# Small memsets between GpSimd's additions, and a new pace for the additions on weights

## The chip, the cores and the metric

The kernel runs on one core of one Trainium2 chip. The metric is the device time of one execution in microseconds (us), the median of several runs. The kernel before took 2261.07 us (median of 3 runs, 2245.42 to 2261.88).

Engines are named as in the profile: PE is TensorE's matmul, PEld its weight load, DVE is VectorE, ACT is ScalarE, POOL is GpSimd, SP is SyncE, whose queue issues nearly all DMAs here. "L141" is line 141 of the kernel file.

## What is computed

Two layers with residuals on `x` of 2 sequences x 2048 tokens x 512, all float32:

```
def _L0_cond_ref(...):
    s0 = relu(x @ swi[0]) @ swo[0]
    s1 = relu(x @ swi[1]) @ swo[1]
    wi_sel = wi[type_label]; wo_sel = wo[type_label]     # one expert per sequence
    h  = relu(einsum('bsd,bdf->bsf', x, wi_sel))
    eo = einsum('bsf,bfd->bsd', h, wo_sel)
    gate_in = concatenate([eo[:, 0], s0[:, 0], s1[:, 0]], -1)
    w = softmax(relu(gate_in @ g1) @ g2)                 # three weights per sequence
    return eo * w[:, 0] + s0 * w[:, 1] + s1 * w[:, 2]

x = x + _L0_cond_ref(...)
x = x + (x @ W[cat_ids] + b[cat_ids])
```

The inner widths are 512 and 2048. Nearly all work lies in the pairs of products `x @ wi` and `h @ wo`.

## The kernel before

**Units and stages.** The tokens are cut into 4 blocks of 1024. A unit is one dense pair on one block: shared expert 0 on four blocks (units 0 to 3), shared expert 1 on four blocks (units 4 to 7), then the chosen expert of sequence 0 (units 8 and 9) and of sequence 1 (units 10 and 11). Each unit has two stages: `up` (the product with `wi`, PE line L803) and `down` (the product with `wo`, PE line L938). Below, "up3" is the up stage of unit 3. In units 9, 10 and 11 the second layer of the blocks that are ready is woven in.

**Products with fewer multiplications.** Every product is done by a two-level Strassen-Winograd scheme: seven outer products instead of eight, and in each of them seven inner ones. Each stage has therefore 49 inner products, of 8 matmuls of 128x256 each: 392 matmuls. The price is sums of blocks of the operands and of the results. Three kinds matter here:

- *Sums on weights* (class `Prep`, additions at L141 through `sums_a`). For each of the six pairs (expert 1, 2, 3) x (wi, wo) there are four groups of 12 additions: four that make `po` (128x384), four `ps` and four `pt` (128x512), read from a raw tile `pr` that four pairs of DMAs load (L179). The sums are stored to DRAM (L228) and loaded later as weights. That is 288 additions on POOL. The sums of expert 0 are made in unit 0 by another class (`First`, L549 and L625), partly on DVE and partly on POOL; the change does not touch it.
- *Sums of x* (`x_sums`, additions at L366 by `outer` and at L380 by `inner`). 36 POOL instructions for each of the units in `MAKES` (0 to 4); PE reads the results (`xi`, `xt`) as moving operands in the same unit's up stage. Units 5 and later load them from DRAM.
- *Sums of h and of the results* on DVE, such as L738 to L745, L781, L909 and L915, whose two inputs both lie in SBUF, and L826 to L850 or L960 to L971, which read one input from PSUM.

**What sets the order.** The schedule is written out by hand: each engine's instructions run in the order in which the program issues them. A stage `up` walks through seven outer products (index `j`, 0 to 6) of 14 slots each; a slot is four matmuls, some 0.86 us of PE time. In each slot the program may issue one step of the sums of x (`advance(xg, 1)`), and then calls `prep_paced(RATE_UP[j])`: the rate is added to a balance (`pace`, at most 4) and each whole unit of the balance issues one addition on weights. With `RATE_UP` (0.36 or 0.24 per slot) a stage issues up to 14 x 2.28 = 31.9 of them. In `down` the rate is 0, and `prep_run` issues two additions at three chosen places (`RUN_DN`); ahead of them it lets POOL wait for a one-element memset of DVE's (`pulse`, L685, read at L686), so that they do not run ahead of their place.

POOL itself knows nothing of slots: it takes its list in order as fast as the data allow. The first addition of each group of 12 waits for its raw tile and for the store of the group before. The raw loads stand in SP's queue between the loads of weight tiles (L479 to L498), which run 12 tiles ahead of PE.

**The x sums in `up`**, by outer product: during `j`=0 the sums for the second outer product are made, during `j`=1 those for the third, and so on; the last (`inner(3)`, used at `j`=6) is issued in slots 7 to 10 of `j`=5.

Of the kernel before, what the change touches and what calls it, by code (L numbers as in the profile page):

```python
# [8 lines left out]
F32 = mybir.dt.float32  # L9
# [6 lines left out]
P = 128  # L16
# [20 lines left out]
def cond_resid_kernel(  # L37
# [22 lines left out]
    nc = tc.nc  # L60
    B, S, D = x.shape
    E, _, F = wi.shape
# [8 lines left out]
    const = ctx.enter_context(tc.tile_pool(name="const", bufs=1))  # L71
# [59 lines left out]
    def sums_a(eng, pick, put):  # L131


        a11, a12, a21, a22 = pick(0, 0), pick(1, 0), pick(0, 1), pick(1, 1)
        for o, i0, i1, op in (
            (put(5), a21, a22, ADD),
            (put(7), a11, a21, SUB),
            (put(6), put(5), a11, SUB),
            (put(3), a12, put(6), SUB),
        ):  # L140
            eng.tensor_tensor(o, i0, i1, op)  # L141
            yield

    class Prep:


# [8 lines left out]
        def begin(self):  # L155
            if not self.todo:
                return
            g = self.todo.pop(0)
            self.since = clock[0]
            e, kind = self.e, self.kind  # L160
            t = bigp.tile([P, 2048], F32, tag="raw", bufs=1, name=f"pr_{e}_{kind}_{g}")

            raw = t.rearrange("p (q b d f) -> p q b d f", q=4, b=2, d=2)
            cols = slice(g * P, (g + 1) * P)
            for c in range(DC):
                if kind == 0 and e < 2:
                    src = swi_v[:, e * DC + c, :, cols]
                elif kind == 0:
                    src = wi_v[:, bass.ds(label[e - 2] * DC + c, 1), :, cols]
                    src = src.rearrange("p o r f -> p (o r) f")  # L170
                elif e < 2:
                    src = swo_v[:, e * 4 + c, g, :].rearrange("p (r f) -> p r f", r=4)
                else:
                    src = wo_v[:, bass.ds(label[e - 2] * 4 + c, 1), g, :]
                    src = src.rearrange("p o (r f) -> p (o r) f", r=4)
                src = src.rearrange("p (c d) f -> p c d f", c=2)
                a, b = divmod(c, 2)
                for k, q in enumerate((1, 2) if a else (0, 3)):
                    nc.sync.dma_start(out=raw[:, q, b, :, :], in_=src[:, k, :, :])  # L179
            place = lambda n: SLOT_A[n] - 4  # L180
            quad = {(0, 0): 0, (1, 0): 1, (1, 1): 2, (0, 1): 3}
            own = {}

            def view(part):
                if part not in own:
                    self.flush(1 << 30, part)
                    own[part] = bigp.tile(
                        [P, 1536 if part == "o" else 2048], F32, tag=part, bufs=1,
                        name=f"p{part}_{e}_{kind}_{g}",
                    )  # L190
                form = {
                    "s": "p (s b d f) -> p s b d f",
                    "o": "p (q s f) -> p q s f",
                    "t": "p (n s f) -> p n s f",
                }[part]
                return own[part].rearrange(form, s=4, f=P, **({"b": 2} if part == "s" else {}))

            def line(part, pick, put):
                gen = sums_a(nc.gpsimd, pick, put)

                def op(k):
                    next(gen)
                    if part != "t":
                        self.reading -= 1
                        self.free = clock[0] + 3
                    if k == 3:
                        self.late.append((clock[0] + 3, part, g, own[part]))

                return [lambda k=k: op(k) for k in range(4)]

            self.p += line(
                "o", lambda r, c: raw[:, 0:3, r, c, :], lambda n: view("o")[:, :, place(n), :]
            )
            self.p += line(
                "s", lambda r, c: raw[:, quad[r, c]], lambda n: view("s")[:, place(n)]
            )
            self.p += line(
                "t", lambda r, c: view("s")[:, :, r, c], lambda n: view("t")[:, :, place(n)]
            )
            self.reading = 8  # L220
# [13 lines left out]
        def step(self):  # L234

            self.flush(clock[0])
            done = self.can()
            if done:
                self.p.pop(0)()
            self.more()  # L240
            return done
# [116 lines left out]
    def x_sums(n):  # L358

        v = [t.rearrange("p b (c d) f -> p b c d f", c=2) for t in xraw[n]]  # L360
        b11, b12, b21, b22 = (v[r][:, :, c] for r in range(2) for c in range(2))
        new = lambda k: topp.tile([P, 4, TQ], F32, tag="top", name=f"x{k}_{n}")

        def outer(o, i0, i1):
            for b in range(2):
                nc.gpsimd.tensor_tensor(o[:, b], i0[:, b], i1[:, b], SUB)  # L366
                yield

        def inner(i, quad):
            t = new(f"i{i}")  # L370
            s = lambda k: t[:, SLOT_B[k] - 4, :]
            pk = lambda r, c: quad[:, r, c, :]
            for k, i0, i1 in (
                (5, pk(0, 1), pk(0, 0)),
                (6, pk(1, 1), s(5)),
                (7, pk(1, 1), pk(0, 1)),
                (4, pk(1, 0), s(6)),
            ):
                x_ops[n, i, k] = s(k)
                nc.gpsimd.tensor_tensor(s(k), i0, i1, SUB)  # L380
                yield
            for k, (r, c) in {1: (0, 0), 2: (1, 0), 3: (1, 1)}.items():
                x_ops[n, i, k] = quad[:, r, c, :]
            parts_of[n, i] = (quad, t)

        sq = lambda t: t.rearrange("p (b d) f -> p b d f", b=2)
        yield from inner(1, b11)
        yield "next"
        if n == 0:
            yield from inner(2, b21)  # L390
            yield "next"
        t1, t2 = sq(new("t1")), sq(new("t2"))
        yield from outer(t1, b12, b11)
        yield from outer(t2, b22, t1)
        yield from inner(6, t2)
        yield "next"
        if n:
            yield from inner(2, b21)
            yield "next"
        yield from inner(5, t1)  # L400
        yield from outer(b12, b22, b12)
        yield "next"
        yield from inner(7, b12)
        yield from outer(b21, b21, t2)
        yield "next"
        yield from inner(4, b21)
        yield "next"
        yield from inner(3, b22)
        yield "next"


    MAKES, LEAVES = range(NB + 1), range(1, NB + 1)
# [239 lines left out]
    def prep_step():  # L652
        done = prep_bg[0].step()
        if prep_bg[0].over():
            prep_bg.pop(0)
        return done
# [3 lines left out]
    def prep_paced(rate):  # L660
        clock[0] += 1
        if prep_bg:
            prep_bg[0].flush(clock[0])
        pace[0] = min(pace[0] + rate, 4.0) if prep_bg else 0.0
        while prep_bg and pace[0] >= 1 and prep_step():
            pace[0] -= 1

    PULSES = 64
    pulse = const.tile([1, PULSES], F32, name="pulse")
    seen = const.tile([1, 1], F32, name="seen")  # L670
    pulses, debt = [0], [0]

    def prep_run(count):

        if not prep_bg:
            return
        debt[0] = min(debt[0] + count, 4) if count else 0
        most = count + 1
        ready = False
        while prep_bg and debt[0] and most:  # L680
            if prep_bg[0].can() and not ready:
                k = pulses[0] % PULSES
                pulses[0] += 1
                mark = pulse[:, k : k + 1]
                nc.vector.memset(mark, 0.0)  # L685
                nc.gpsimd.tensor_tensor(seen, mark, mark, ADD)  # L686
                ready = True
            if not prep_step():
                break
            debt[0] -= 1  # L690
            most -= 1
# [56 lines left out]
    def up(n, xg, tops, y):  # L748
# [12 lines left out]
        for j, i in enumerate(I_UP(n)):  # L761
# [32 lines left out]
            for s, (bk, k, d) in enumerate(SEQ_UP):  # L794
# [76 lines left out]
                    done = advance(xg, 1)  # L871
                if s in top_at:
                    next(tg, None)
                prep_paced(RATE_UP[j])
                if n or j or s >= 4:
                    step(other_bg)
                if s == 4 and n not in MAKES and j + 2 < NP:
# [9 lines left out]
    def down(n, H, tops, y, prepare):  # L887
# [124 lines left out]
        for s, (i, name) in enumerate(SLOTS_DN):  # L1012
# [12 lines left out]
            prep_paced(0.0)  # L1025
            prep_run(RUN_DN.get((i, name), 0))
            step(other_bg)
# [195 lines left out]


    RATE_UP = [0.36, 0.36, 0.36, 0.36, 0.24, 0.24, 0.36]
    RUN_DN = {(7, "x6"): 2, (4, "x6"): 2, (4, "y5"): 2}

    with tc.manual_schedule():
# [18 lines left out]
        for n, (e, blk) in enumerate(units):  # L1247
# [4 lines left out]
            if n:  # L1252
                y = yp.tile([P, DC, 4, TQ], F32, tag="y", name=f"y_{n}")
            H = up(n, xg, tops, y)
            coming = {}

# [82 lines left out]
```

## Time and profile before

| | |
|---|---|
| median of 3 runs | 2261.07 us (2245.42 to 2261.88) |
| the profiled execution | 2258.7 us, of which the span of the program is 2256.9 us |
| PE busy | 2196.7 us, 9808 matmuls |
| DVE busy | 1647.6 us |
| POOL busy | 753.6 us, 616 instructions |
| granted TensorE clock, mean | 0.995 |

The span is one execution as the hardware profiler recorded it, from the first instruction to the last; 1.8 us of the execution's own time lie around it. A timeline row gives start, length, engine, line, operation, output and inputs, and in brackets how long the engine had been idle before and what ended that.

### The profile page before, as it was taken

The page shows a single profiled execution, that of the slowest core. Times are in us where ns is not written, and L with a number is a line of the kernel's source. Part 1 is how long each engine was busy: PE and PEld are TensorE (multiplying, and loading weights), DVE is VectorE, ACT ScalarE, POOL GpSimd, SP SyncE. Part 2 cuts the span into 40 slices and gives each one's busy share as a digit, 9 for nine tenths or more (in the row PEclk, how much of TensorE's full clock was granted, in tenths as well). Part 3 has the DMA queues.
Part 4 walks back from the last instruction along what each step waited for, and adds up shares of the span by engine and source line. Part 5 has one row for each costly group of instructions (what it writes and reads, how often), then busy time and mean ns, then how long its engine had stood idle before and what let it go on. Part 6 is the DMA issues. An engine that isn't in the chain of part 4 may idle for free.

```text
span 2256.9 us, 28576 instructions
## 1 busy us (share of the span) xinstructions
PE 2196.7 (97%) x9808; PEld 1850.6 (82%) x9808; DVE 1647.6 (73%) x2028; ACT 544.4 (24%) x937; POOL 753.6 (33%) x616
## 2 busy tenths in 40 slices
PE   8899998999999999999999999999999999999999
PEld 6787887888888878888888888888777877887786
DVE  7897778587688597587587687587676746767685
ACT  3321230331231231131141141131133133113310
POOL 5787523550850750240350340330032023002300
PEclk9999999999999999999999999999999999999999
DMA  9553996997997896896897896895896597579671
GB/s 339 202 182 119 340 305 204 306 320 239 306 328 231 284 321 191 295 312 207 297 311 217 270 335 213 277 339 173 294 292 189 186 315 232 152 245 321 212 276 56
DMA packets 483339, 577.22 MB, mean 256 GB/s; under 512 B 28280, under 2 KB 316024, under 8 KB 479740
## 3 DMA queue, kind: packets, MB, share of 16 engines
q1 hardware_dynamic: 479468, 568.58, 77.4%
q10 hardware_dynamic: 3728, 6.82, 0.9%
q8 instruction: 80, 1.31, 0.2%
q14 instruction: 63, 0.52, 0.1%
HBM read 417.47 MB, written 157.81 MB: 255 GB/s over the span
## 4 chain that ended last, share of the span: by engine, by line
PE 61%; DVE 5%; DMA 2%; POOL 1%; issue 0%; ACT 0%; SPq 0%; DVEq 0%; POOLq 0%; ACTq 0%
PE dx L938 18%; PE ux L803 14%; PE dy L938 9%; PE uy L803 7%; PE po L1119 5%; PE dz L938 5%; PE uz L803 3%; DVE h L781 1%; DMA w<-ws_s 1%; DMA g1raw<-in_L_cond_g_dram 1%; DVE hid L1059 1%; DVE us L826 1%; DVE h L850 1%; POOL xi L380 0%; DVE acc L1197 0%
## 5 line engine op out<-in xcount | busy, mean ns | idle before, releaser
L938 PE MATMUL dx<-t,w 128*128 128x256 f32 x1680 | 399.4, 381 | 14.4 <-DVE ds L960 14.4
L803 PE MATMUL ux<-xs,w 128*128 128x256 f32 x1568 | 377.1, 381 | 10.4 <-DVE sm L1082 3.1
L938 PEld LDWEIGHTS dx<-t,w 128*128 128x128 f32 x1680 | 319.1, 191 | 60.5 <-DVE ds L960 15.1
L803 PEld LDWEIGHTS ux<-xs,w 128*128 128x128 f32 x1568 | 295.0, 190 | 67.3 <-DVE us L826 9.6
L1156 POOL TENSOR_TENSOR mix<-mix 128x512 f32<-128x512 f32 x72 | 101.4, 1408 | 525.4 <-ACT mix L1151 521.7
L826 DVE TENSOR_TENSOR us<-ux,h 128x512 f32<-128x512 f32 x240 | 162.3, 684 | 118.3 <-PE ux L803 117.8
L909 DVE TENSOR_TENSOR h<-h,h 128x1024 f32<-128x1024 f32 x192 | 240.9, 1269 | 0.0
L775 ACT ACTIVATE h<-h 128x1024 f32<-128x1024 f32 x156 | 164.4, 1055 | 240.3 <-DVE h L831 112.8
L803 PE MATMUL ux<-xi,w 128*128 128x256 f32 x808 | 194.7, 384 | 11.0 <-DVE us L826 4.5
L831 DVE TENSOR_TENSOR h<-uy,us 128x512 f32<-128x512 f32 x168 | 115.9, 691 | 111.4 <-ACT us L824 107.1
L803 PE MATMUL uy<-xs,w 128*128 128x256 f32 x784 | 187.8, 380 | 3.4 <-DVE h L850 3.1
L837 ACT ACTIVATE h<-uz 128x512 f32<-128x512 f32 x168 | 99.4, 592 | 379.6 <-PE uz L803 360.6
L803 PEld LDWEIGHTS ux<-xi,w 128*128 128x128 f32 x808 | 153.1, 192 | 38.2 <-issue 13.1
L803 PEld LDWEIGHTS uy<-xs,w 128*128 128x128 f32 x784 | 148.3, 190 | 30.2 <-DVE h L850 6.2
L686 POOL TENSOR_TENSOR seen<-pulse 1x1 f32<-1x1 f32 x18 | 10.9, 605 | 474.0 <-DVE pulse L685 474.0
L938 PE MATMUL dy<-h,w 128*128 128x256 f32 x672 | 160.5, 382 | 4.6 <-DVE y L962 4.6
L141 POOL TENSOR_TENSOR po<-pr 128x384 f32<-128x384 f32 x48 | 52.8, 1115 | 312.2 <-DMA w<-ws_s 124.4
L781 DVE TENSOR_TENSOR h<-h,h 128x1024 f32<-128x1024 f32 x96 | 149.8, 1561 | 6.2 <-ACT h L837 4.9
L850 DVE TENSOR_TENSOR h<-uy,us 128x512 f32<-128x512 f32 x168 | 112.8, 686 | 51.0 <-PE uy L803 48.8
L938 PEld LDWEIGHTS dy<-h,w 128*128 128x128 f32 x672 | 128.1, 191 | 23.6 <-issue 5.2
L938 PE MATMUL dz<-h,w 128*128 128x256 f32 x616 | 145.6, 379 | 0.1
L938 PE MATMUL dx<-h,w 128*128 128x256 f32 x616 | 145.5, 379 | 0.0
(155 smaller groups left out, 3442.2 us busy)
## 6 DMA issues: line engine op xcount, KB each, us to landing
w<-ws_t SPq DMA_DIRECT2D x352, 256.0 KB, 4.2
w<-ws_s SPq DMA_DIRECT2D x270, 256.0 KB, 4.4
w<-ws_o SPq DMA_DIRECT2D x264, 256.0 KB, 4.9
xs<-xs SPq DMA_DIRECT2D x49, 896.0 KB, 7.0
ws_s<-ps SPq DMA_DIRECT2D x24, 1024.0 KB, 7.3
ws_t<-pt SPq DMA_DIRECT2D x24, 1024.0 KB, 7.8
ys<-y SPq DMA_DIRECT2D x11, 2048.0 KB, 8.0
ws_o<-po SPq DMA_DIRECT2D x24, 768.0 KB, 7.8
```

What stands on the lines that cost most here:

```text
L141: eng.tensor_tensor(o, i0, i1, op)
L775: nc.scalar.activation(v, v, AF.Relu)
L781: nc.vector.tensor_tensor(o, blk_of(O[22], cc), blk_of(O[21], cc), ADD)
L803: nc.tensor.matmul(p[:, g, :], lhsT=wt[:, 2 * d + g, :], rhs=x_ops[n, i, k], start=first and g == 0, stop=True, skip_group_check=True,)
L826: nc.vector.tensor_tensor(t, p, half(src, 12 if k == 6 else 22, d), ADD)
L831: nc.vector.tensor_tensor(half(dst, 22, d), bank["y", d], t, ADD)
L837: nc.scalar.activation(half(dst, 11, d), p, AF.Relu if i in final else AF.Copy)
L850: nc.vector.tensor_tensor(half(dst, 12, d), p, sn["b", d], ADD)
L909: nc.vector.tensor_tensor(bl(o), bl(i0), bl(i1), SUB)
L938: nc.tensor.matmul(p, lhsT=wt[:, g, :], rhs=op[g], start=first and g == 0, stop=True, skip_group_check=True,)
L1119: nc.tensor.matmul(po[t], lhsT=mixed[c], rhs=l1[blk][0][:, c, :], start=(c == 0), stop=(c == DC - 1),)
L1156: nc.gpsimd.tensor_tensor(m[:, 3, :, :], m[:, 3, :, :], m[:, j, :, :], ADD)
```

## The change

A memset of 64 elements per partition is issued on POOL once or several times behind its additions: four behind each addition on weights of `Prep`, one behind each addition of the sums of x. All of them write the same tile `idle`, which nobody reads. In units that make sums of x (0 to 4), `up` takes its rates from a new list `RATE_X`, with 0 in the first outer product. The ring of DVE's pulses shrinks from 64 to 16 elements.

```diff
+    idle = const.tile([P, 64], F32, name="idle")
+
+    def rest(count):
+        for _ in range(count):
+            nc.gpsimd.memset(idle, 0.0)
...
                 def op(k):
                     next(gen)
+                    rest(4)
                     if part != "t":
                         self.reading -= 1
                         self.free = clock[0] + 3
...
         def outer(o, i0, i1):
             for b in range(2):
                 nc.gpsimd.tensor_tensor(o[:, b], i0[:, b], i1[:, b], SUB)
+                rest(1)
                 yield
...
                 x_ops[n, i, k] = s(k)
                 nc.gpsimd.tensor_tensor(s(k), i0, i1, SUB)
+                rest(1)
                 yield
...
-    PULSES = 64
+    PULSES = 16
...
-                prep_paced(RATE_UP[j])
+                prep_paced((RATE_UP if n not in MAKES else RATE_X)[j])
...
     RATE_UP = [0.36, 0.36, 0.36, 0.36, 0.24, 0.24, 0.36]
+    RATE_X = [0.0, 0.36, 0.42, 0.42, 0.36, 0.36, 0.42]
```

## The prediction

> **What bounds the kernel now.** I read the page first, then the busy time by stage, then PE's waits and the timeline around the longest of them.
>
> ```profile
> span 2256.9 us, 28576 instructions
> PE 2196.7 (97%) x9808; PEld 1850.6 (82%) x9808; DVE 1647.6 (73%) x2028; ACT 544.4 (24%) x937; POOL 753.6 (33%) x616
> ```
>
> PE is busy 97% of the span, so a change to POOL can only shorten or lengthen the stretches in which PE waits. The table by stage shows where these are (columns: stretch, its length, busy time and instructions of PE, PEld, DVE, ACT, POOL, then clock, DMA share, GB/s).
>
> ```profile
> 210.90:298.80 87.90, 85.91 (x394) 74.02 (x393) 62.01 (x80) 29.44 (x42) 61.08 (x54) 1.00 0.96 316
> 298.80:400.20 101.40, 90.47 (x425) 79.01 (x424) 76.68 (x79) 15.22 (x41) 24.68 (x27) 0.95 0.71 229
> 575.40:662.50 87.10, 85.35 (x393) 74.05 (x392) 68.73 (x80) 29.35 (x42) 71.17 (x65) 1.00 1.02 336
> 748.70:839.90 91.20, 87.53 (x394) 75.15 (x393) 67.69 (x79) 29.28 (x42) 68.64 (x64) 0.98 1.00 327
> 839.90:924.50 84.60, 84.60 (x394) 74.48 (x393) 62.79 (x76) 10.00 (x25) 0.27 (x1) 1.00 0.69 211
> ```
>
> The last row, down4, has almost no POOL work and is solid PE: 392 matmuls in 84.6 us, 0.216 us each. That is the floor of a stage. Above it lie up1 3.3, down1 13.3 (101.4 less 84.6 and less 32 transposes of 0.109), up2 2.4, up3 2.5, down3 1.6, up4 6.6, up5 1.4, up6 2.9, up8 1.7 (their windows: 87.0, 87.1, 86.2, 91.2, 86.0, 87.5, 86.3). Down1's loss is a single wait. These are DVE's, POOL's and PE's rows of it:
>
> ```profile
> 379.58 14.55 DVE L915 TENSOR_TENSOR y<-y 128x512 f32<-128x512 f32 x1
> ...
> 391.92 0.98 POOL L141 TENSOR_TENSOR po<-pr 128x384 f32<-128x384 f32 x1
> 392.87 0.71 POOL L380 TENSOR_TENSOR xi<-xt 128x256 f32<-128x256 f32 x1
> 393.66 1.05 POOL L380 TENSOR_TENSOR xi<-xt,xi 128x256 f32<-128x256 f32 x1
> ...
> 394.52 3.78 PE L938 MATMUL dx<-t,w 128*128 128x256 f32 x8 [10.93 <-DVE ds L960]
> ```
>
> A DVE addition that takes 0.69 us elsewhere took 14.55. POOL's rows from 379.55 to 393.58 stand end to end, each beginning some 0.03 us before the one ahead has ended; the first gap is the 0.08 us from 393.58 to 393.66, and DVE's row ends 0.5 us later. So a DVE addition with both inputs in SBUF gets nowhere while POOL's additions follow without a gap, and a gap of 0.08 us is enough to let it in. PE lost 10.9 us, and its next eight matmuls took 3.78 us instead of the usual 1.89. Up4 shows the same: L738, usually 1.22 us, ran from 786.94 to 794.34 until POOL paused 0.84 us for a DMA.
>
> ```profile
> 786.94 7.40 DVE L738 TENSOR_TENSOR y<-h 128x1024 f32<-128x1024 f32 x1 [1.12 <-ACT h L775]
> ...
> 794.10 1.37 POOL L366 TENSOR_TENSOR x<-x,xt 128x512 f32<-128x512 f32 x1 [0.84 <-DMA xs<-x]
> ```
>
> The Trainium skill (SBUF — State Buffer, Who interferes with whom) says that a DVE instruction with two SBUF inputs contends with a GpSimd one that reads SBUF, that whichever starts first keeps the shared ports for the whole instruction, and that one that only writes does not contend. Read literally, DVE would wait for one addition, 1.25 us at most; the measured 14.55 us contradicts that, and by the literal rule the memsets would recover nothing, giving 2258.7 + 9.5 = 2268 us.
>
> **The change part by part.** All sums start from the profiled 2258.7 us (span 2256.9 and 1.8 around it). The median is 2.4 us above it, while the fastest run, 2245.42, lies 13.3 below, which is just what down1's wait costs; whether that run lacked the wait no view shows.
>
> *What a memset costs.* No memset of this size is in the trace; the nearest rows are these:
>
> ```profile
> 0.25 0.10 POOL L1324 MEMSET const-float32-0.0<- 128x1 f32 x1 [0.25 <-issue]
> 0.28 0.10 POOL L1324 MEMSET const-float32-1.0<- 128x1 f32 x1
> ...
> 0.74 0.20 POOL masks.py:197 MEMSET ident<- 128x128 f32 x1 [0.29 <-POOLq L1324]
> 1.02 0.29 POOL masks.py:199 TENSOR_SCALAR_AFFINE_SELECT ident<-ident 128x128 f32<-128x128 f32 x1
> ```
>
> One element takes 0.10 us and 128 take 0.205, so 64 take about 0.15. Independent ones start 0.03 us apart, an overlap of 0.065; then four cost 4 x 0.087 = 0.35. A dependent operation starts 0.08 us after the end of the other (1.02 against 0.945; 393.66 above). All memsets write one tile, so I expect each to be held behind the one before: 4 x 0.15 + 3 x 0.08, less 0.04 of overlap with the addition = 0.80 us per addition on weights. A pulse read (L686 at 743.04) that shares only its output with the one before it carries a wait on POOL's own count, which is why I take the upper value. One memset behind a sum of x costs 0.11.
>
> *What POOL gains in load.* 288 x 0.80 + 180 x 0.11 = 250 us on top of 753.6, nearly all before up9. In up5 to up8 POOL is busy 37 to 42 of 85 us and 31 additions add 25: covered. In up1 to up4 `RATE_X` issues 14 x 2.34 = 32.8 additions against 31.9, none in the first outer product. There 33 x 0.80 + 32 x 0.11 = 30 us come on top of 57 to 71 us of 87. Queued behind the rests are the sums of x, and PE waits for these. Up1 shows how near it is:
>
> ```profile
> 252.44 0.99 POOL L141 TENSOR_TENSOR po<-pr 128x384 f32<-128x384 f32 x1 [22.28 <-DMA xs<-xt]
> ...
> PE ux L803 <- POOL xi L380: 0.9, 1, 0.9
> PE uy L803 <- POOL xi L380: 0.4, 1, 0.4
> ```
>
> POOL stands still for 22 us until a group's raw tile lands, and then works through nine additions and seven sums before the first sum of `inner(4)` ends at 274.67, just when PE takes it (274.72, after a wait). With rests, the nine additions take 7.2 us more. Against that, five rows of that stretch are lengthened by about 1 us each by DVE, some 4 us of which fall into the rests; and five additions per stage fewer lie ahead, since the first outer product issues none. I put the loss at 3 us in up1 and up2 (the latter has the same slack of 0.1 us at `inner(4)`), 2 in up3 (slack 0.1 us only at its last sums), 1 in up4 (slack 9 to 16 us): **+9**. The bounds: 0, if POOL's own idle time absorbs it, and 15.6 per stage, if nothing does. The latter is the demand, 33 x (1.17 + 0.80) + 24 x 0.83 + 8 x 1.37 + 5 of contention = 100.6, less 85: 62 us in four stages.
>
> *What DVE gains.* With a rest behind each addition DVE waits for one addition at most. Down1: 13.3 less 1 left over, **-12.3**. Up4: 6.6 less 1.1 (POOL's share and small rows), **-5.5**. Down3, where L915 took 4.25 us instead of 0.69: **-1**. Up5, up6 and up8, whose waits are on L820, L826 and L850 behind delayed DVE sums: half of 6.0, **-3**. Single PE stops with no releaser in up1 to up3 (about 4 us, beside busy POOL): half, **-2**. Together -23.8; at the most all that lies above the floor in these stages, 35.7. At the least 0.
>
> *Unit 0.* 36 rests of 0.11 are 4 us of POOL. Only the first two sums of x are tight (PE takes them 0.1 and 0.7 us after they end); later ones have 5 us or more. **+0.5**; bounds -3 (PE waits there too for L826, 5.4 us with stage down0 and up1) and +4. Down0's waits stay: POOL's L625 and L549 there get no rests.
>
> *Edits at nothing.* 18 pulses in a ring of 16: the seventeenth reuses a place read over 1000 us earlier. SP's stores of sums (L228) wait for POOL, 25 us now, and weight loads queue behind them; twelve tiles of 1.73 us less 4.9 us to land cover 16 us of lateness. If that cover is gone, each further microsecond is PE's.
>
> Sum: 2258.7 - 23.8 + 0.5 + 9 = **2244**.
>
> **The rivals.**
> 1. *The rests fill POOL up* (slower). Place: the sums of x in up1 to up4. Price: 62 us less the gain of 24, so 2258.7 + 0.5 + 62 - 24 = 2297. It decides once four memsets cost more than POOL has to spare: 14 us idle or more per stage, shared by 33 additions, 0.42 us. For it: my 0.80 is above that. Against it: five to seven additions come after the last sum of x and can spill into `down`, where POOL works 12 of 85 us, and the contention partly disappears into the rests.
> 2. *The rests are short and the sums come in time.* Four memsets at 0.35 stay below the 0.42: the gain of 24 without the 9, and POOL's waits (1.3 us in up1) gone as well: about 2234, at the lowest 2258.7 - 35.7 = 2223. Against it: the wait at 743.04.
> 3. *The memsets hold DVE off as additions do.* Then back-to-back rows stay back-to-back, nothing is gained, the 9.5 us are paid, and the 4 us of contention that I let fall into the rests come back: 2272. Against it: a 0.08 us gap sufficed at 393.6, and dependent memsets leave three such.
>
> **How the numbers follow.** Forecast 0.50 (2236 to 2256), first rival 0.12, second 0.30, third 0.08. The range of 8 in 10 reaches from 2228, inside the second rival, to 2272, the third; what is left out is the first rival and the lower end of the second. About 1% is what a measurement of this kernel can tell from no change: 2238.5 and 2283.7 around the median. Faster by over 1%: most of the second rival and a little of the forecast, 0.32. Slower: most of the first, 0.10. Within: 0.58.
>
> **What would show it.** Right: no DVE row of several us in down1 and up4 (L915, L738), those stages at 89 to 90 and 86 to 87 us, POOL's memsets at 0.15 us and 0.2 us apart, POOL busy near 980 us, PE's waits on `xi` (L380) grown to 5 to 12 us in up1 to up3. Wrong: waits on `xi` of tens of us, or waits of SP on POOL with PE behind them; L915 or L738 as long as before; memset rows 0.03 us apart; or down1 gaining nothing because other stages of the changed kernel starve in its place.

## The result, and the profile after

| | before | after |
|---|---|---|
| median | 2258.56 us (6 runs, 2245.42 to 2261.88) | 2296.14 us (6 runs, 2291.26 to 2299.37) |
| ratio | | 1.0158, 95% interval 1.0135 to 1.0181 |
| profiled execution, span | 2256.9 us | 2297.6 us |

The changed kernel is slower by 1.6%; the forecast was 2244, in a range of 2228 to 2272. The lines of the changed kernel's file stand 8 to 10 lower than before: L803 is L813 there, L380 is L389, L366 is L374, L915 is L925, and the memsets are L149. Its page, the first lines, and the group of the memsets:

```profile
span 2297.6 us, 29888 instructions
...
PE 2210.0 (96%) x9808; PEld 1863.0 (81%) x9808; DVE 1621.5 (71%) x2031; ACT 544.9 (24%) x937; POOL 909.4 (40%) x1951
...
L149 POOL MEMSET idle<- 128x64 f32 x1332 | 200.8, 151 | 49.5
```

1332 memsets (288 x 4 + 180) of 0.151 us each fill 201 us. POOL's busy time grows by 156 only, since its rows overlap a little at their ends and its additions take 12 us less. DVE has 26 us less to do; its four longest rows of before (14.55, 7.40, 4.25 and 3.56 us) held as much in delay. The table by stage (columns as in the prediction) shows up1, down1, up2, up3, up4 and up6:

```profile
215.40:308.10 92.70, 87.55 (x394) 75.80 (x393) 58.76 (x80) 29.43 (x42) 70.46 (x188) 0.96 0.92 304
308.10:396.20 88.10, 88.10 (x426) 77.52 (x425) 67.05 (x79) 15.22 (x41) 18.46 (x48) 1.00 0.83 261
396.20:495.40 99.20, 87.72 (x394) 76.17 (x393) 58.81 (x79) 29.42 (x42) 85.78 (x217) 0.93 0.89 288
583.90:687.80 103.90, 90.64 (x394) 77.97 (x393) 60.53 (x80) 29.39 (x42) 90.26 (x224) 0.92 0.87 284
772.70:867.20 94.50, 88.20 (x393) 76.22 (x392) 62.13 (x79) 29.39 (x42) 86.33 (x220) 0.96 0.95 311
1122.20:1218.80 96.60, 89.38 (x394) 76.26 (x393) 60.00 (x79) 29.52 (x42) 56.96 (x163) 0.96 0.99 316
```

Down1 has gone from 101.4 to 88.1 us, its floor. But up1 to up4 have gone from 353.3 together to 390.3, and up6 from 87.5 to 96.6. PE's waits, and the longest of them on PE's and POOL's timelines in up2:

```profile
PE uy L813 <- POOL xi L389: 34.6, 5, 11.5
...
PE ux L813 <- POOL idle L149: 5.8, 5, 2.7
...
PE ux L813 <- DMA w<-ws_s: 3.6, 2, 3.2
```

```profile
456.84 1.89 PE L813 MATMUL ux<-x,w 128*128 128x256 f32 x8
470.21 2.07 PE L813 MATMUL uy<-xi,w 128*128 128x256 f32 x4 [11.48 <-POOL xi L389]
```

```profile
447.86 0.99 POOL L141 TENSOR_TENSOR po<-pr 128x384 f32<-128x384 f32 x1 [8.26 <-DMA w<-ws_s]
448.79 0.78 POOL L149 MEMSET idle<- 128x64 f32 x4
449.52 1.27 POOL L141 TENSOR_TENSOR po<-pr 128x384 f32<-128x384 f32 x1
...
467.50 1.26 POOL L141 TENSOR_TENSOR pt<-ps 128x512 f32<-128x512 f32 x1
468.70 0.78 POOL L149 MEMSET idle<- 128x64 f32 x4
469.43 0.72 POOL L389 TENSOR_TENSOR xi<-x 128x256 f32<-128x256 f32 x1
```

A group of additions on weights begins at 447.86, when its raw tile has come (the last part landed at 447.55; the row names another load). Nine of them, each with its four memsets, stand ahead of the first sum of `inner(4)` (469.43), and PE stands 11.5 us for that sum. Before, waits on `xi` were 1.7 us in all, and none of PE's waits was ended by a memset; the second row's 5.8 us lie in unit 0 but for 0.5.

### The profile page after: what moved, and what is told of

It is laid out like the page before. It is cut to its first block, busy times and chain, and to the rows that moved or that the text cites. A ratio compares the mean times of both kernels' runs of the same rounds, so it can differ in the third digit from the quotient of the medians.

```text
span 2297.6 us, 29888 instructions
## 1 busy us (share of the span) xinstructions
PE 2210.0 (96%) x9808; PEld 1863.0 (81%) x9808; DVE 1621.5 (71%) x2031; ACT 544.9 (24%) x937; POOL 909.4 (40%) x1951
## 4 chain that ended last, share of the span: by engine, by line
PE 75%; DVE 8%; POOL 5%; DMA 4%; issue 1%; SPq 1%; ACT 0%; POOLq 0%; DVEq 0%; ACTq 0%
PE dx L948 22%; PE ux L813 18%; PE dy L948 11%; PE uy L813 9%; PE dz L948 6%; PE po L1129 5%; PE uz L813 4%; DVE h L919 1%; POOL idle L149 1%; POOL po L141 1%; POOL ps L141 1%; DMA w<-ws_s 1%; DMA g1raw<-in_L_cond_g_dram 1%; DVE h L791 1%; POOL xi L389 1%
## 5 line engine op out<-in xcount | busy, mean ns | idle before, releaser
L813 PE MATMUL ux<-xs,w 128*128 128x256 f32 x1568 | 380.8, 384 | 19.4 <-DMA w<-ws_s 3.6
L813 PEld LDWEIGHTS ux<-xs,w 128*128 128x128 f32 x1568 | 297.0, 191 | 77.6 <-issue 16.9
L919 DVE TENSOR_TENSOR h<-h,h 128x1024 f32<-128x1024 f32 x192 | 246.1, 1297 | 0.0
L149 POOL MEMSET idle<- 128x64 f32 x1332 | 200.8, 151 | 49.5
L813 PE MATMUL ux<-xi,w 128*128 128x256 f32 x808 | 196.7, 387 | 9.2 <-POOL idle L149 5.8
L813 PE MATMUL uy<-xs,w 128*128 128x256 f32 x784 | 188.9, 382 | 2.5 <-DVE h L860 2.3
L813 PEld LDWEIGHTS ux<-xi,w 128*128 128x128 f32 x808 | 156.4, 195 | 35.8 <-POOL idle L149 7.7
L813 PEld LDWEIGHTS uy<-xs,w 128*128 128x128 f32 x784 | 149.5, 191 | 29.4 <-DVE h L860 4.7
L791 DVE TENSOR_TENSOR h<-h,h 128x1024 f32<-128x1024 f32 x96 | 136.8, 1425 | 6.4 <-ACT h L847 5.1
```

The costliest lines, as they stand in the source:

```text
L149: nc.gpsimd.memset(idle, 0.0)
L791: nc.vector.tensor_tensor(o, blk_of(O[22], cc), blk_of(O[21], cc), ADD)
L813: nc.tensor.matmul(p[:, g, :], lhsT=wt[:, 2 * d + g, :], rhs=x_ops[n, i, k], start=first and g == 0, stop=True, skip_group_check=True,)
L919: nc.vector.tensor_tensor(bl(o), bl(i0), bl(i1), SUB)
```

## The experiments

A rest is the memset or the memsets behind one addition. Theory A: the time of the rests makes sums of x late in up1 to up4. Theory B: the new pace does. The other question is what lets DVE in.

**e1: the old pace, all rests.**

```diff
-                prep_paced((RATE_UP if n not in MAKES else RATE_X)[j])
+                prep_paced(RATE_UP[j])
```

> The changed kernel with the old rates in the up stages of units 0 to 4 again; all rests stay. Theory A (the time of the rests on weights, 0.67 us per addition, makes the sums of x late): the waits for sums of x remain, 30 us or more, time 2285 to 2315. Theory B (the new pace, which packs the additions into outer products 1 to 6, makes them late): the waits fall below 10 us, time 2245 to 2260.

2292.52 us, ratio 1.0148 (1.0130 to 1.0167). Up1 to up4 take 393.0 us, PE's waits on the sums of x are 32.3: A. But up5 to up8 are back at 342.8 (358.3 with the new pace), so the loss there needs the new pace.

**e2: the new pace, no rests** (the kernel before with `RATE_X`).

```diff
-                prep_paced(RATE_UP[j])
+                prep_paced((RATE_UP if n not in MAKES else RATE_X)[j])
...
+    RATE_X = [0.0, 0.36, 0.42, 0.42, 0.36, 0.36, 0.42]
```

> The kernel before with the new rates in the up stages of units 0 to 4, and no rests. Theory A: the waits for sums of x stay at a few us, time 2240 to 2265, depending on whether a DVE addition still starves behind POOL somewhere. Theory B: waits for sums of x of 25 us or more, time 2275 to 2300.

2275.4 us, ratio 1.0078 (1.0056 to 1.0100): slower, which A did not expect and B expected, though with less waiting than B asked for:

```profile
PE uy L803 <- POOL xi L380: 9.6, 3, 5.1
```

In its trace up1 to up4 are 361.7, up5 to up8 350.2. So the pace costs time without any rest. The traced execution is the fastest of e2's four, 10 us under its median, and no view shows what the others lost beyond it.

**e3: one memset instead of four, new pace.**

```diff
-                    rest(4)
+                    rest(1)
```

> The changed kernel with one memset instead of four behind each addition on weights; the rest of the change stays. Theory A: one memset costs about 0.1 us, so the sums of x are in time again (PE waits for them under 8 us) and weights too (up6 and up7 within 3 us of the floor), while DVE still gets in behind each addition: down1 stays near 88 us. Time 2235 to 2252. Theory C (DVE gets in only through the gaps that a chain of dependent memsets leaves): long DVE rows of over 3 us come back, down1 at 95 us or more in the trace, time 2250 to 2265.

2264.13 us, ratio 1.0008 (0.9994 to 1.0022). Dropping three memsets brings 32 us back; up1 to up4 fall from 390.3 to 368.3. The rest of what A expected fails: the time, the waits on sums of x (17.4 us, not under 8), and up6 and up7, which stay at 94.3 and 89.2, as the pace would have it. Of theory C nothing is left: no addition of DVE's takes over 2.4 us after unit 0.

**e4: no memsets behind additions on weights, new pace.**

```diff
-                    rest(4)
```

> The changed kernel without the memsets behind additions on weights; one behind each sum of x and the new pace stay. Theory A: no lateness of sums of x or weights, but DVE can starve behind runs of additions on weights: time 2240 to 2262, DVE rows over 3 us in the trace. Theory B: as slow as the changed kernel, 2285 or more.

2262.48 us, ratio 1.0009 (0.9995 to 1.0023). Up1 to up4 362.7 and up5 to up8 349.6, as in e2's trace, although e2's median is 13 us higher. PE still waits 13.6 us for sums of x, so A's "no lateness" fails here too, and B's 2285 as well; additions of DVE's of 3.0 to 3.4 us are back.

**e5: one memset behind each addition, old pace.**

```diff
-                    rest(4)
+                    rest(1)
...
-                prep_paced((RATE_UP if n not in MAKES else RATE_X)[j])
+                prep_paced(RATE_UP[j])
```

> One memset behind each addition on weights and each sum of x, with the old pace. Theory A (time of the rests in the up stages): three memsets less per addition are 0.57 us; up1 to up4, 393 us with four memsets and this pace, come to 350 to 358 (353 in the kernel before, 368 with one memset and the new pace), down1 stays near 88, up6 and up7 near 87 and 85: time 2238 to 2252. Theory A2 (no rest of any size pays, because each sum of x is just in time already): up1 to up4 at 362 or more, time 2255 to 2265.

2244.25 us, ratio 0.9946 (0.9925 to 0.9967): faster than the kernel before. Up1 to up4 are 353.0, down1 88.1, waits on sums of x 6.3.

**e6: as e5, without the memsets behind the sums of x.**

```diff
                 nc.gpsimd.tensor_tensor(o[:, b], i0[:, b], i1[:, b], SUB)
-                rest(1)
...
                 nc.gpsimd.tensor_tensor(s(k), i0, i1, SUB)
-                rest(1)
```

> As the run before it, but without the memsets behind the sums of x: one memset behind each addition on weights, old pace. If the rests behind the sums of x cost nothing, within 4 us of that run; if 180 x 0.11 us of them stand in PE's way in part, 3 to 10 us less, the most of it in up1 to up4. If DVE needs them to get in between sums of x that follow each other, DVE rows over 3 us come back and the time is 5 to 15 us more.

2244.27 us, ratio 0.9942 (0.9920 to 0.9964). The memsets behind the sums of x make no difference in time; up1 to up4 are 350.5, and no long DVE addition comes back.

**e7: four memsets, but only behind the additions issued in `down`; old pace.** `rest(resting[0])` stands behind the addition, with 0 elsewhere.

```diff
-            if not prep_step():
+            resting[0] = 4
+            done = prep_step()
+            resting[0] = 0
+            if not done:
```

> Four memsets behind the additions on weights that are issued in the down stages, none elsewhere, old pace. Theory A: a rest costs nothing where POOL has time: up1, up2, up3 as before (87 to 89), up6 and up7 as before, and L915's long wait in down1 is gone (88 to 90); up4 keeps its own wait or not by chance (86 to 92). Time 2238 to 2252. If a rest in down only moves the wait into the next stage, down1 falls and up2 grows by 5 or more: 2252 to 2262.

2244.3 us, ratio 0.9942 (0.9922 to 0.9962). 140 memsets (35 additions) do what the 1332 were to do: down1 88.1, up1 to up4 349.7.

**e8: the pause alone** (the kernel before with `RATE_X = [0.0, 0.36, 0.36, 0.36, 0.24, 0.24, 0.36]`).

```diff
-                prep_paced(RATE_UP[j])
+                prep_paced((RATE_UP if n not in MAKES else RATE_X)[j])
```

> The kernel before with rate 0 in the first outer product of units 0 to 4 and the old rates after it (27 instead of 32 additions per stage); no rests. Of the loss of the new pace (up2 and up3 up by 12 us together, up6 and up7 by 7), theory B1 puts it on the pause, which moves each group's start some 8 us later, so that the raw tile's wait falls ahead of tight sums of x: up2 and up3 then stay at 180 us or more together. Theory B2 puts it on the denser additions after the pause: up2 and up3 fall to 175 us or less, as before or better. Time 2245 to 2262 in B2, 2260 to 2280 in B1.

2269.23 us, ratio 1.0049 (1.0033 to 1.0064). Up2 and up3 are 85.9 and 86.0: B2, the pause does not make sums of x late, the denser additions behind it do. The time, above B2's range, went elsewhere. Seven additions are left over for up9; the stores of their sums wait ahead of the gate's first load (`g1raw`) in SP's queue, which is issued 13.3 us into up9 instead of 1.1 (the stage takes 130.0 us instead of 119.1). And DVE starves in down2 now, seen on DVE's timeline and POOL's:

```profile
560.71 13.07 DVE L915 TENSOR_TENSOR y<-y 128x512 f32<-128x512 f32 x1
```

```profile
572.51 0.71 POOL L380 TENSOR_TENSOR xi<-xt 128x256 f32<-128x256 f32 x1
573.30 1.06 POOL L380 TENSOR_TENSOR xi<-xt,xi 128x256 f32<-128x256 f32 x1
```

The signature is that of down1 before: DVE gets in at the first gap (573.22 to 573.30) after 12.5 us of POOL rows end to end.

**e9 and e10: two and three memsets, old pace** (`rest(2)` and `rest(3)` in e1's kernel).

> Two memsets behind each addition on weights, one behind each sum of x, old pace. Measured so far with this pace: one memset (0.09 us per addition) leaves up1 to up4 at 353 us, four (0.71) at 393; two cost 0.09 + 0.21 = 0.29. Theory D1 (POOL has some 0.4 us per addition to spare, and only what goes beyond it is PE's): up1 to up4 353 to 357, time 2240 to 2250. Theory D2 (each microsecond of rest reaches PE in proportion): 366, time 2252 to 2260.

> Three memsets (0.50 us per addition), the rest as in the run with two. D1: 0.08 us beyond what POOL can spare, of the 0.29 by which four go beyond it: up1 to up4 360 to 368, time 2247 to 2262. D2: 380, time 2265 to 2275.

e9 2263.6 us, ratio 1.0014 (1.0002 to 1.0025); e10 2279.37, 1.0079 (1.0049 to 1.0109). Up1 to up4: 372.3 and 388.5. D1 falls, and D2 is still too low. With e5 and e1 the ratios to the kernel before, each from runs side by side, are 0.9946, 1.0014, 1.0079 and 1.0148 for one to four memsets: each further memset costs 0.65 to 0.7%, some 15 us. (The medians alone, 2244.3, 2263.6, 2279.4 and 2292.5, come from three rounds in which the kernel before itself had 2257.7 to 2262.3.) A memset lengthens POOL's list in up1 to up4 by 124 additions x 0.21 = 26 us, so somewhat more than half of a rest's time reaches PE from the second memset on. Meanwhile POOL still stands idle (pauses over 0.2 us) for 49 us of these four stages in e9, 41 in e10 and 27 in e1, of 92 before: most of that idle time is no reserve.

**e11: four short memsets, each on its own tile, old pace.**

```diff
-    idle = const.tile([P, 64], F32, name="idle")
+    idle = [const.tile([P, 16], F32, name=f"idle_{k}") for k in range(4)]
...
-        for _ in range(count):
-            nc.gpsimd.memset(idle, 0.0)
+        for k in range(count):
+            nc.gpsimd.memset(idle[k], 0.0)
```

> Four memsets of 16 elements behind each addition on weights and one behind each sum of x, each of the four on its own tile so that none waits for the one before; old pace. If the chain on one tile is what makes four memsets cost 0.71 us, these start 0.04 to 0.1 us apart and cost 0.2 to 0.4 us together: up1 to up4 353 to 362, time 2242 to 2256. If a memset costs 0.2 us whether it waits or not: up1 to up4 near 390, time 2280 or more.

2246.0 us, ratio 0.9931 (0.9907 to 0.9955). These memsets take 0.108 us and start 0.046 apart (0.208 in the chain), and the next addition starts 0.15 us after the end of the one before instead of 0.67. Up1 to up4 are 359.4. It is mostly the chain that made four memsets dear: their smaller size saves at most 4 x 0.043 = 0.17 of these 0.52 us.

**e12: four memsets in `down` and in up5 to up8, none in up0 to up4 or behind sums of x; old pace.**

```diff
-                    rest(4)
+                    rest(resting[0])
...
-                rest(1)
...
-                rest(1)
...
-                prep_paced((RATE_UP if n not in MAKES else RATE_X)[j])
+                resting[0] = 0 if n in MAKES else 4
+                prep_paced(RATE_UP[j])
+                resting[0] = 4
```

> Four memsets behind the additions on weights that are issued in down stages and in up5 to up8, none in up0 to up4 and none behind the sums of x; old pace. Theory A (the loss lies in up1 to up4, where sums of x queue behind the rests): up5 to up8 within 4 us in all of the kernel before (344.5), up1 to up4 350 as with rests in down only, time 2238 to 2250. If rests also make weights late in up6 and up7 by themselves: up5 to up8 at 355 or more, 2252 to 2262.

2242.29 us, ratio 0.9915 (0.9891 to 0.9939). Up5 to up8 are 343.7: full rests cost nothing where no sums of x are made. Its interval overlaps those of e5, e6, e7 and e11; all five beat the kernel before, and which is best is not decided.

## Why the prediction was wrong

The profiled spans differ by 40.7 us. By stages, from the traces (us). The traced executions of e1 and e2 are 8 and 10 us under the medians of their kernels, so that these two columns are low by some us:

| | before | e2: pace | e12: rests elsewhere | e5: one memset | e1: four, old pace | after |
|---|---|---|---|---|---|---|
| start, up0, down0 | 210.9 | 216.1 | 214.9 | 212.2 | 212.1 | 215.4 |
| up1 to up4 | 353.3 | 361.7 | 349.3 | 353.0 | 393.0 | 390.3 |
| down1 to down4 | 360.3 | 348.0 | 345.9 | 346.3 | 345.5 | 346.2 |
| up5 to up8 | 344.6 | 350.2 | 343.7 | 344.2 | 342.8 | 358.3 |
| the rest | 987.8 | 987.5 | 988.4 | 986.0 | 989.4 | 987.5 |

**What DVE gains** was right in its mechanism and its largest term. Down1 to down4 gain 14.1 us (forecast 13.3), and L915's row in the changed kernel (minimum, median, maximum in ns) no longer has a long one; below it the same row of e5, with one memset:

```profile
L925 DVE TENSOR_TENSOR y<-y x96: 680/691/1782, 193.4 to 2258.8; 128x512 f32<-128x512 f32 x96
```

```profile
L925 DVE TENSOR_TENSOR y<-y x96: 681/691/1782, 190.2 to 2203.0; 128x512 f32<-128x512 f32 x96
```

In all ten kernels with memsets behind the additions on weights in `down`, no DVE addition behind unit 0 took over 2.4 us; in the four without (before, e2, e4, e8) the longest took 14.6, 4.3, 3.4 and 13.1. Where the starvation falls differs from kernel to kernel: e2, without a memset, has down1 at 88.4. In e7 and e12 up1 to up4 have no memsets, so that up4's long L738 is absent there without any. The up stages gain less than the 10.5 forecast: at best 4.0 in up1 to up4 (e12) and 3.0 in up5 to up8 (e9).

**The price of the memsets** was mis-sized a little: 0.71 us instead of 0.80 for four, 0.09 instead of 0.11 for one. The dependence on one tile was right; the step is 0.208 us, with a gap of 0.06.

**The step that failed** is "I put the loss at 3 us in up1 and up2 [...], 2 in up3 [...], 1 in up4: +9". It measured +37, or +41 against e12, which has no rests there. The +9 lies near the lower bound, and two of the grounds for that gave way.

- "0, if POOL's own idle time absorbs it" does not hold. Of the changed kernel's 37 us of pauses in up1 to up4, 33 lie ahead of a group's first addition, which waits for a raw tile whose load comes at PE's time, and the tight sums come right behind it. E9 and e10 show more than half of a rest's time at PE while POOL still idles for 41 to 49 us.
- "Five additions per stage fewer lie ahead, since the first outer product issues none" was an error. Between the group's start and `inner(4)` stand seven additions in up1 (nine before) and nine in up2 (ten before), since the rates behind the pause are denser. And the group starts later: 48.3 us into up1 (41.6 before) and 51.7 us into up2 (41.8 before); with the new pace and no rests (e2) it is 49.1 and 50.0.

The third ground, contention that falls into the rests, held in part: the time by which POOL's additions exceed their usual length in up1 to up4 fell from 34 to 23 us.

The wait in up2 can be split. In e2 the same nine additions stand there without rests, and PE waits 3.6 us; with rests it waits 11.5. Of the 7.9 us between, nine rests of 0.71 are 6.4, and the group starts 1.7 later. With no rests the new pace costs up1 to up4 8.4 us (e2); the four rests with the old pace cost 43.7 over e12 (e1). The two do not add: together they cost 41, and the ratios (1.0078, 1.0148, and 1.0158 for both) do not add either.

**The first rival**, 2297, came nearest the time. It priced up1 to up4 at 62 and decided at 0.42 us of rest per addition; 41 was measured, and 0.42 is no threshold: up1 to up4 are 353 us at 0.09 us of rest per addition (e5), 359 at 0.18 (e11) and 372 at 0.29 (e9). That its time fits is luck in part: it had 21 us too much in these stages, nothing for the 14 us that up5 to up8 lost, and a gain of 24 where down1 to down4 gave 14. I had weighed it at 0.12 although my own price of a rest stood above its limit. (The terms of its demand, as written, add up to 100.9, not 100.6.)

**Edits at nothing** is the second term that failed. Weights are late in up6 and up7, which are 14.5 us longer together; 9.5 us of that are PE's waits for weight tiles. These are the rows in up6:

```profile
1168.30 3.63 PE L813 MATMUL ux<-xs,w 128*128 128x256 f32 x8 [2.89 <-DMA w<-ws_t]
...
1204.92 1.46 PE L813 MATMUL ux<-xs,w 128*128 128x256 f32 x5 [3.18 <-DMA w<-ws_s]
```

It is the pace that brings this about: with the old pace up6 and up7 stay at 87.7 and 84.8 under all four rests (e1); with the new one they are 91.6 and 87.5 without any (e2), 94.3 and 89.2 with one memset (e3), and 96.6 and 90.2 with four. Both kernels use the same rates in these stages, but the groups start elsewhere: with the new pace three raw tiles are loaded in up6, at 5, 33 to 38 and 70 us, with the old one two. The number of loads alone does not explain it: up5 of the changed kernel and up6 of e8 load three as well, and PE waits for no weights there (85.6 and 85.5 us). SP's waits for sums to store grew from 30 to 94 us, but they are 107 in e1, where PE waits 1.5 us for weights in up6 and up7. What delays the weights stays open.

**Unit 0** (+0.5 forecast) is 4.5 us longer, but this stretch varies from 210.0 to 216.1 us over the fourteen traces without following the rests (216.1 in e2, which has none), so its length is not put down to them. PE does wait 5.3 us there for POOL's rows L149, and for none of POOL's before; its waits on DVE are shorter in turn, and all its waits in up0 come to 13.7 us against 11.9.

## What to carry to other kernels

A pause that is to let one engine in delays everything queued behind it on the engine that takes it; here somewhat more than half of each further memset's time reached PE. Give it only where nothing urgent is queued behind (four memsets behind the 35 additions issued in the down stages, e7, brought as much as one behind all 288, e5), and make it as short as works, here one memset. Idle time of an engine ahead of a late input is no reserve for work behind that input; count slack from the input's arrival to the next urgent result. A pace that is moved shifts the groups' loads in all later stages, and those belong to its price.

## What was not expected of the hardware

One memset behind an addition lets DVE's two-input additions in although POOL's rows leave no gap, but it did not keep a small copy of DVE's from a long wait. In e5, on POOL's and DVE's timelines:

```profile
569.71 0.98 POOL L141 TENSOR_TENSOR po<-po,pr 128x384 f32<-128x384 f32 x1
570.64 0.14 POOL L149 MEMSET idle<- 128x64 f32 x1
570.75 1.26 POOL L374 TENSOR_TENSOR xt<-x 128x512 f32<-128x512 f32 x1
```

```profile
567.99 5.37 DVE L1046 COPY gin<-y 128x4 f32<-128x4 f32 x1
```

The copy takes 0.16 us where it is not held up, 5.37 here, and 0.56 at most in the changed kernel, whose chained memsets leave gaps. In the kernel before the same copy took 7.38 us at 575.90, until POOL's first gap.

This fits what the Trainium skill (SBUF — State Buffer, Who interferes with whom) says: a GpSimd instruction that only writes does not contend with a DVE instruction with two SBUF inputs, while a DVE copy in a 2-port mode contends with GpSimd. Whether this copy runs in such a mode no run shows. Its statement that the one that starts first keeps the ports for one instruction falls short in two kernels without memsets: in e8 and in the kernel before, the wait of L915 lasts until POOL's list has a gap, 13.1 and 14.6 us.

PE's granted clock was lower in the stages with long waits: up3 of the changed kernel, with 13.1 us of waiting on sums of x, was granted 0.92 (1.00 before), and eight matmuls behind the wait of 2.89 us at 1168.30 took 3.63 us instead of 1.89, 1.7 us on top of the wait.
